# A four-layer graph network on one core: several joined edits, and an order planned with shorter delays

## The chip, the core and the metric

One core of a Trainium2 chip runs the whole program: TensorE (PE, with its weight loads PEld), VectorE (DVE), ScalarE (ACT), GpSimd (POOL) and SyncE (SP), which issues most DMAs. Each engine takes its instructions strictly in the order in which they stand in the program. The metric is the device time in microseconds of one execution; a median over several runs is given, and the profile shows one execution more.

## The reference, cut to what matters

The input x has 128 graphs of 64 nodes with 256 features, all with the same 64 x 64 adjacency adj. Four layers, each closed by a residual and a plain layer norm, all in f32:

```
x = LN(x + L0(x)); x = LN(x + L1(x)); x = LN(x + L2(x)); x = LN(x + L3(x))
L0: A_hat = D^-1/2 (adj + I) D^-1/2;  h = relu(BN((A_hat x) W1' + b1));  out = BN(h W2' + b2)
L1: Chebyshev-like: L_norm = 2 adj / (lam_max + 1e-8) - I, lam_max the largest eigenvalue of adj
    x1 = relu(LN((L_norm x) Wc + bc)) + x;  4-head attention masked by adj > 0;  LN;  GELU MLP;  LN
L2: two graph convolutions with relu, then for p = 1..4 an LSTM over windows of p nodes;
    the last state of each window replaces the node p-1 of the window
L3: Wh = h W;  e = leaky_relu(s1_i + s2_j), s1 = Wh a1, s2 = Wh a2, masked where adj == 0;
    softmax over j;  out = attention Wh
```

BN means over all 8192 rows, so layer 0 has two points at which every block must be done before any goes on.

## The kernel before, in words

The rows are cut into 16 blocks of 512 (eight graphs, as four tiles of 128 rows: `NT = 4`), and the blocks into four groups of four (`NG = 4`). A block is a [128, 1024] slab in SBUF, either row-major (`tm`) or feature-major (`fm`); TensorE transposes change one into the other (`to_fm`, `to_tm`). PSUM holds four slabs (`PS`), and eight spare slabs (`mem`), joined later by slabs that are no longer needed, carry what lives between two steps.

The program is not written in the order in which it runs. Each piece of work is a generator (`first_block`, `eig`, `second_block`, `end_block`, `block`, `gcn_block`, `unit`, which calls `lstm`, and `last_block`), and before each group of instructions it yields a `step`: the engine (T, V, S, G, or Q for SP's DMA queue), the planned duration, the PSUM slabs and the spare slabs that it takes, and, with `at`, the time at which its inputs are planned to be there. `flow` (lines 127-200) keeps a clock per engine, and picks again and again the step that can begin earliest, where MARGIN is added to the ready time of a step on T, V or S, and ties go to the stream with the lower priority number. A task's next step is planned 0.2 us after the end of the one before (`best[3] = end + 0.2`); where `at` is used, the body adds 0.2 by hand. What comes out is the order of instructions on each engine. Streams have a width: how many of their tasks may be open at once.

What the steps below touch:

- Start (lines 238-427): the four quadrants of `bdA` and `bdAT` (adj and its transpose twice on a diagonal) are loaded on SP in turn, `adj2` twice on ACT's queue, then x's first block and W1T on ACT's queue, W2T and six small columns on SP. VectorE makes the masks `cap1` and `cap3` and the degree `dinv`, and TensorE the matrix `AhT`, which the first aggregation (`aggregate`) waits for.
- `eig` (lines 432-487): 26 squarings of a 128 x 128 matrix for lam_max, spread between the matmuls of layer 0; `LnT` comes of it.
- Layer norms: `stats` (four times bn_stats and bn_aggr, then + EPS, lines 269-278), the power -1/2 on POOL, and then in `ln_steps` four VectorE operations (line 288), in `ln_steps_act` one small VectorE operation and four ScalarE ones (line 316), in `ln_affine_steps` eight VectorE ones.
- `end_block` ends layer 0, `block` is layer 1; both end with `ln_steps`. `gcn_block` is the convolutions of layer 2 with p = 1.
- `unit` runs p = 2, 3, 4 on a group, or part of it. Its first window step is plain. In the further steps the products of [x, h] with the weights use a seven-product form with sums of blocks (`product` at line 1000, stages 1 to 4): fewer columns on TensorE, and more copies and sums on ScalarE, VectorE and POOL. p = 4 of the last group is done as two units of 16 windows by 16 graphs (256 columns); all other units of p = 4 have 512.
- `last_block` (layer 3, lines 1269-1376) is done per block: add, norm, transpose, Wh (line 1308), e as 16 matmuls on quadrants of the array (1327, 1330), ScalarE 0.2 e (1337), VectorE max, mask, row maximum, subtraction (1340-1344), exp (1346), row sums and reciprocal, POOL's scaling (1352), transpose (1358), the product with Wh (1366), add (1370), norm, store.

In the second plan the streams are, from the most urgent: lending of slabs, small loads, weights, `last_block` of the last group (width 4), gcn (2), layers 0 end and 1 (6), units (2), `last_block` of the other groups (2).

Of the kernel before, what the change touches and what calls it, by code (L numbers as in the profile page):

```python
# [15 lines left out]
P = 128  # L16
# [3 lines left out]
NT = 4  # L20
# [7 lines left out]
EPS = 1e-5  # L28
MARGIN = {"T": 2.0, "V": 0.5, "S": 0.5}
# [3 lines left out]
def kernel(ctx: ExitStack, tc: tile.TileContext, a: dict, out: bass.AP):  # L33
# [93 lines left out]
    def flow(streams, margin):  # L127
# [8 lines left out]
        while True:  # L136
# [55 lines left out]
            best[5] += sl  # L192
            if waits:
                best[3] = end + 0.2
            try:
                best[2] = best[1].send(end)
# [43 lines left out]
    for s in range(2):  # L240
        h = halves[s]
        nc.sync.dma_start(bdA[h, h], a["adj"])
        nc.sync.dma_start(bdAT[h, h], a["adjT"])
        nc.scalar.dma_start(adj2[h, :], a["adj"])
        for m in (bdA, bdAT):
            G.memset(m[h, halves[1 - s]], 0.0)
# [9 lines left out]

    cap1 = ctile([P, N], "cap1")
    V.tensor_scalar(cap1, adj2, 0.0, BIG, ALU.is_gt, ALU.mult)
    V.tensor_scalar(cap1, cap1, -1.0e9, None, ALU.add)

    cap3 = ctile([P, N], "cap3")
    V.tensor_scalar(cap3, adj2, 0.0, 2.0, ALU.not_equal, ALU.mult)
    V.tensor_scalar(cap3, cap3, -1.0, BIG, ALU.add, ALU.mult)

# [4 lines left out]
    def stats(y, n=NT):  # L269

        st = sm.tile([P, n, 6], F32, tag="ln_st", name="ln_st")
# [8 lines left out]
    def ln_steps(y):  # L280

        yield step("V", 2.7)
# [9 lines left out]
    def ln_affine_steps(y, g, b):  # L292

        yield step("V", 2.7)
# [10 lines left out]
    def ln_steps_act(y):  # L305

        yield step("V", 2.7)
        mv, rs = stats(y)
        yield step("G", 1.0)
        G.tensor_tensor(rs, rs, neghalf[:, :NT], ALU.pow)  # L310
        yield step("V", 0.2)
        nm = sm.tile([P, NT], F32, tag="ln_nm", name="ln_nm")
        V.scalar_tensor_tensor(nm, mv[:, :, 0], -1.0, rs, ALU.mult, ALU.mult)  # L313
        yield step("S", 2.4)
        for t in range(NT):
            S.activation(  # L316
                y[:, t, :], y[:, t, :], AF.Identity, scale=rs[:, t : t + 1], bias=nm[:, t : t + 1]
            )
# [13 lines left out]
    def to_fm(ps, y):  # L332

        for c in range(2):
            for t in range(NT):
                T.transpose(ps[:, c, t * P : (t + 1) * P], y[:, t, c * P : (c + 1) * P], ident)

    def to_tm(ps, yT):

        for t in range(NT):  # L340
# [48 lines left out]
    with c0:  # L389
        ep = c0.enter_context(tc.tile_pool(name="eig", bufs=2))  # L390

        first = mem.take()
        nc.scalar.dma_start(tm(mem[first]), x_blk[0])
        W1T = load_w(wp, "W1T", a["L0_gnn_W1"], queue=nc.scalar)
        W2T = load_w(wp, "W2T", a["L0_gnn_W2"])
        cols = {k: load_col(wp, f"l0{k}", a[f"L0_gnn_{k}"]) for k in ("b1", "g1", "be1", "b2", "g2", "be2")}
# [11 lines left out]

        An = ctile([P, P], "An", wp)
        V.tensor_tensor(An, bdA, ident, ALU.add)  # L410
        tmp = etile("etmp")
        V.tensor_tensor(tmp, bdAT, ident, ALU.add)
        d3 = etile("d3", 3, 1)
        V.reduce_sum(d3[:, 0:1], An, axis=AX.X)
        V.reduce_sum(d3[:, 1:2], tmp, axis=AX.X)
        tmp = etile("etmp")
        V.tensor_tensor(tmp, An, ident, ALU.mult)
        V.reduce_sum(d3[:, 2:3], tmp, axis=AX.X)
        dinv = etile("dinv", 1, 1)
        V.tensor_tensor(dinv, d3[:, 0:1], d3[:, 1:2], ALU.add)  # L420
        V.tensor_tensor(dinv, dinv, d3[:, 2:3], ALU.subtract)
# [10 lines left out]
        def eig():  # L432
            Sy = etile("Sy", bufs=1)
            yield step("V", 1.2)
            V.tensor_tensor(Sy, bdA, bdAT, ALU.add)
# [75 lines left out]
        def first_block(i):  # L511
            if i:
# [3 lines left out]
            else:  # L516
                xs = first
            yield step("T", 1.9, ps=1, sl=1)
# [4 lines left out]
            yield step("V", 1.3, ps=-1)  # L523
# [3 lines left out]
            for hf in range(2):  # L527
                dst = fm(Xs[i]) if hf == 0 else H[i]
                yield step("T", 3.5, ps=1)
# [9 lines left out]
                yield step("V", 1.3, waits=hf == 1)  # L539
# [4 lines left out]
        def second_block(i):  # L544
# [5 lines left out]
            yield step("T", 7.0, ps=1)  # L550
# [14 lines left out]
            yield step("V", 1.3)  # L565
# [5 lines left out]
        tasks = [(None, lambda: first_block(0), 1), (None, eig, 0)]  # L571
        tasks += [(None, lambda i=i: first_block(i), 2) for i in blocks if i]
# [45 lines left out]
    def end_block(i):  # L618
# [9 lines left out]
        yield step("T", 1.0, ps=1)  # L628
# [3 lines left out]
        yield step("V", 1.3, ps=-1)  # L632
# [3 lines left out]
        yield from ln_steps(x)  # L636
        mark("end", i)

    def block(i):
        x = X[i]  # L640
        mark("begun", i)
        yield step("T", 1.9, ps=1, sl=1)
# [3 lines left out]
        yield step("S", 1.1, ps=-1)  # L646
        S.copy(mem[s_xp], PS[ps])
        PS.give(ps)
        yield step("T", 3.5, ps=1, sl=1)
# [4 lines left out]
        yield step("V", 1.3, ps=-1)  # L654
# [4 lines left out]
        yield step("V", 1.3)  # L659
        V.scalar_tensor_tensor(y, y, 0.0, x, ALU.max, ALU.add)  # L660

        yield step("T", 1.0, ps=1, sl=1)
# [3 lines left out]
        yield step("S", 1.1, ps=-1)  # L666
# [4 lines left out]
        for w in (Wq, Wk):  # L671
            yield step("T", 3.5, ps=1, sl=1)
# [3 lines left out]
            yield step("S", 1.1, ps=-1, waits=False)  # L676
# [23 lines left out]
        yield step("S", 1.1, ps=-1, waits=False)  # L700
# [8 lines left out]
        yield step("T", 1.9, ps=1, sl=1)  # L709
# [26 lines left out]
        yield step("S", 1.1, tbl="exp")  # L736
# [9 lines left out]
        yield step("T", 1.0, ps=1, sl=1)  # L746
# [6 lines left out]
        yield step("S", 1.1, ps=-1)  # L753
# [20 lines left out]
        yield step("S", 1.1, ps=-1)  # L774
        S.copy(mem[s_o], PS[ps])
        PS.give(ps)
        yield step("T", 3.5, ps=1)
# [3 lines left out]
        yield step("V", 1.3, ps=-1)  # L781
# [5 lines left out]
        yield step("T", 1.0, ps=1, sl=1)  # L787
# [14 lines left out]
        for hf in range(2):  # L802
            yield step("T", 3.5, ps=1, sl=1)
# [14 lines left out]
        yield step("T", 7.0, ps=1)  # L818
# [12 lines left out]
        yield step("V", 1.3, ps=-1)  # L831
# [4 lines left out]
        yield from ln_steps(x)  # L836
# [13 lines left out]
    av = load_w(gw, "av", a["L3_gnn_a"])  # L850
    bl = load_col(gw, "bih", a["L2_gnn_bih"])
# [3 lines left out]
    def gcn_rows():  # L855
# [5 lines left out]
        yield step("T", 1.0, ps=1)  # L861
# [40 lines left out]
    def lstm(p, n, parts, x_of, out_of):  # L902
# [38 lines left out]
        def gates(pair, t, ps, sl):  # L941
            t = yield step("S", 0.1 + n * 2.5e-3, ps=-1, at=t + 0.2, waits=False, tbl="sigmoid")
# [15 lines left out]
        for c in range(2):  # L958
# [3 lines left out]
            t = yield step("G", g_us, at=t + 0.2, waits=False)  # L962
# [567 lines left out]
```

## Time and profile before

| | us |
|---|---|
| runs shown: median (lowest to highest) | 2455.06 (2454.82 to 2457.53) |
| profiled execution: its own time | 2454.4 |
| profiled execution: span on the core | 2452.6 |
| TensorE busy | 2353.9 |
| VectorE busy | 1274.4 |
| ScalarE busy | 1095.9 |
| GpSimd busy | 572.8 |
| mean granted TensorE clock | 0.982 of full speed |

In the profile L12 is line 12 of the kernel; lines of helpers (L324 aggregate, L342 and L336 transposes, L348 and L360 weight products) stand for all their callers. In a table by stage each row has the stretch, its length, then busy us and number of instructions of PE, PEld, DVE, ACT and POOL, the granted clock, the DMA share and GB/s. In the list of waits a row reads "engine, what it was to compute and its line <- what it waited for: us in total, times, longest". In a timeline a row has the start, the time taken, the engine, the line, the operation, and the idle time before it in brackets. Ends of matmuls are modelled; their starts are what to count with.

### The profile page before, as it was taken

What the parts mean: (1) busy time and instruction counts of PE and PEld (TensorE: products, weight loads), DVE (VectorE), ACT (ScalarE), POOL (GpSimd) and SP (SyncE); (2) the same over time, 40 slices, a digit from 0 to 9 for tenths busy, and PEclk for the clock granted to TensorE, in tenths of its full rate; (3) what the DMA queues carried; (4) which work ended last, traced back from release to release, by engine and by line L of the source; (5) the groups of instructions that cost most, each with busy time, mean ns of one, the idle gap of its engine ahead of it and who ended that gap; (6) DMA issues with size and microseconds to landing.
All of it is one profiled execution on the core that took longest, in us unless ns stands there. A gap on an engine that the chain in (4) does not pass through costs nothing. (4 is left out here: it accounts for less than half of the span.)

```text
span 2452.6 us, 35349 instructions
## 1 busy us (share of the span) xinstructions
PE 2353.9 (96%) x14468; PEld 1818.8 (74%) x14468; DVE 1274.4 (52%) x2965; ACT 1095.9 (45%) x1916; POOL 572.8 (23%) x416
## 2 busy tenths in 40 slices
PE   8999888999999999999999999999999999999986
PEld 5544466767667767675766888899999889888874
DVE  4542387657455645484552433345344455455664
ACT  2256332333444343434434444445435465556774
POOL 0000034233323222343132222222222221222211
PEclk9999899999999999999999999999999999999997
DMA  5110110100000000000100000000000010000111
GB/s 171 43 52 0 40 36 27 44 3 15 1 9 10 18 9 10 1 9 35 44 26 11 16 1 1 1 18 1 1 1 18 1 35 10 26 18 18 61 53 44
DMA packets 40499, 57.60 MB, mean 23 GB/s; under 512 B 4624, under 2 KB 33936, under 8 KB 40336
## 3 DMA queue, kind: packets, MB, share of 16 engines
q1 hardware_dynamic: 39376, 54.25, 6.8%
q8 instruction: 113, 1.85, 0.3%
q10 hardware_dynamic: 960, 1.08, 0.1%
q14 instruction: 50, 0.41, 0.1%
HBM read 38.55 MB, written 16.78 MB: 23 GB/s over the span
## 5 line engine op out<-in xcount | busy, mean ns | idle before, releaser
L1000 PE MATMUL ps<-x,x 128*128 128x256 f32 (+1 forms) x1024 | 228.4, 360 | 0.0
L1000 PEld LDWEIGHTS ps<-x,x 128*128 128x128 f32 x1024 | 179.8, 190 | 19.5 <-DVE t L1046 0.4
L1000 PE MATMUL ps<-t,x 128*128 128x256 f32 (+1 forms) x800 | 178.5, 359 | 1.4 <-ACT x L1040 1.4
L1000 PEld LDWEIGHTS ps<-t,x 128*128 128x128 f32 x800 | 140.5, 190 | 18.9 <-ACT x L1040 2.0
L932 PE MATMUL ps<-h,wL 128*128 128x144 f32 (+2 forms) x552 | 131.8, 393 | 0.0
L348 PE MATMUL ps<-t,W1T 128*128 128x512 f32 x256 | 116.0, 597 | 0.0
L932 PEld LDWEIGHTS ps<-h,wL 128*128 128x128 f32 x552 | 87.9, 190 | 37.7 <-issue 36.8
L285 POOL TENSOR_TENSOR ln_rs<-ln_rs,neghalf 128x4 f32<-128x4 f32 x48 | 49.6, 1033 | 202.1 <-DVE ln_rs L277 202.0
L944 ACT ACTIVATE t<-ps,bih 128x512 f32<-128x512 f32 (+3 forms) x116 | 68.5, 642 | 57.7 <-PE ps L932 57.6
L275 DVE BATCH_NORM_STATS2 ln_st<-x 128x6 f32<-128x256 f32 x240 | 92.0, 403 | 0.7
L1059 DVE COPY x<-ps 128x256 f32<-128x256 f32 (+3 forms) x84 | 30.7, 366 | 118.6 <-PE ps L1000 118.5
L297 POOL TENSOR_TENSOR ln_rs<-ln_rs,neghalf 128x4 f32<-128x4 f32 x32 | 36.6, 1145 | 230.9 <-DVE ln_rs L277 230.8
L1076 ACT ACTIVATE x<-x,bih 128x512 f32<-128x512 f32 (+3 forms) x84 | 53.1, 632 | 77.9 <-DVE x L1066 77.7
L932 PE MATMUL ps<-h,x 128*128 128x256 f32 x384 | 87.1, 379 | 0.8 <-ACT t L1152 0.8
L1000 PE MATMUL ps<-h,x 128*128 128x256 f32 (+1 forms) x416 | 84.4, 333 | 1.1 <-DVE x L1059 0.6
L932 PEld LDWEIGHTS ps<-h,x 128*128 128x128 f32 x384 | 72.7, 190 | 10.9 <-ACT t L1152 1.2
L348 PEld LDWEIGHTS ps<-t,W1T 128*128 128x128 f32 x256 | 46.2, 191 | 45.9 <-issue 45.9
L288 DVE TENSOR_SCALAR x<-x,ln_mv,ln_rs 128x256 f32<-128x256 f32 x144 | 63.3, 495 | 31.5 <-POOL ln_rs L285 31.5
L1066 DVE TENSOR_TENSOR x<-ps,x 128x512 f32<-128x512 f32 (+3 forms) x84 | 48.5, 579 | 57.4 <-PE ps L1000 46.1
L1076 ACT ACTIVATE t<-t,bih 128x512 f32<-128x512 f32 (+3 forms) x59 | 36.9, 629 | 86.1 <-DVE t L1066 85.9
L944 ACT ACTIVATE x<-ps,bih 128x512 f32<-128x512 f32 (+3 forms) x88 | 51.6, 639 | 50.2 <-PE ps L932 50.1
L276 DVE BATCH_NORM_AGGREGATE ln_mv<-ln_st 128x2 f32<-128x6 f32 x448 | 71.5, 166 | 0.0
(663 smaller groups left out, 5691.6 us busy)
## 6 DMA issues: line engine op xcount, KB each, us to landing
t<-in_x_dram SPq DMA_DIRECT2D x25, 512.0 KB, 4.0
xd<-x SPq DMA_DIRECT2D x16, 512.0 KB, 2.6
x<-xd SPq DMA_DIRECT2D x8, 512.0 KB, 3.3
out_dram<-x SPq DMA_DIRECT2D x8, 512.0 KB, 2.9
h<-in_x_dram SPq DMA_DIRECT2D x6, 512.0 KB, 4.1
t<-xd SPq DMA_DIRECT2D x6, 512.0 KB, 3.3
out_dram<-t SPq DMA_DIRECT2D x6, 512.0 KB, 2.9
wL<-in_L_gnn_Wih_dram SPq DMA_DIRECT2D x2, 1024.0 KB, 5.0
```

The lines of the kernel that those rows point to most:

```text
L275: V.bn_stats(st[:, t, :], y[:, t, :])
L276: V.bn_aggr(mv[:, t, :], st[:, t, :])
L285: G.tensor_tensor(rs, rs, neghalf[:, :NT], ALU.pow)
L288: V.tensor_scalar(y[:, t, :], y[:, t, :], mv[:, t, 0:1], rs[:, t : t + 1], ALU.subtract, ALU.mult)
L297: G.tensor_tensor(rs, rs, neghalf[:, :NT], ALU.pow)
L348: T.matmul(ps[:, c, :], w[:, k, (off + c) * P : (off + c + 1) * P], yT[:, k, :], start=(k == 0), stop=(k == nk - 1),)
L932: T.matmul(spread(fm(PS[ps])[:, j, :n], q), WL[p][0][:, k, m], x_of(0, q)[:, k], start=(k == 0), stop=(k == 1),)
L944: S.activation(of(sl)[:, j], fm(PS[ps])[:, j, :n], AF.Tanh if g == 2 else AF.Sigmoid, bias=bias(g, c))
L1000: T.matmul(dst, WS[p][name](k, g), y[:, k], start=first and k == 0, stop=k == 1, skip_group_check=not first)
L1059: V.tensor_copy(y[:, 1, :], v[:, 0, :])
L1066: V.tensor_tensor(y[:, 0:2, :], v[:, 2:4, :], y[:, 0:2, :], ALU.add)
L1076: S.activation(of(act[g])[:, 0], of(act[g])[:, 0], f, bias=bias(g, 0))
```

## The change

1. Planner: `end + 0.2` becomes `end + lag`, 0.2 after a step on T and 0.06 after any other; the 0.2 that the bodies added by hand are gone, since `send` now gives `end + lag`. Many planned durations are a little shorter.
2. Start: bdAT is loaded on ACT's queue; adj2 is summed from the halves of bdA instead of loaded; three blocks of x are loaded ahead (SP, ACT, SP); all columns but b1, and W2T, are loaded by a task of their own (`later_loads`), which also makes the masks; the degree comes of two operations with an accumulated row sum.
3. `end_block` and the last norm of `block` use `ln_steps_act`.
4. Units of 16 graphs (the last two) run `plain_steps` instead of the seven-product form.
5. `last_block` can do part of a block; the last group is done in halves of two tiles. e comes of two matmuls over the whole array: block-diagonal ones times a diagonal made by POOL, and the identity times a broadcast column. leaky_relu is one VectorE operation after the mask, the subtraction of the maximum is the bias of exp, the row sums are accumulated by exp, and the division comes with the last add.
6. Streams: the last two units have a stream of their own, and `last_block` of the first three groups has width 4.

```diff
+LAG, LAG_T = 0.06, 0.2
...
+            lag = LAG_T if e == "T" else LAG
             if waits:
-                best[3] = end + 0.2
+                best[3] = end + lag
             try:
-                best[2] = best[1].send(end)
+                best[2] = best[1].send(end + lag)
...
-        nc.sync.dma_start(bdAT[h, h], a["adjT"])
-        nc.scalar.dma_start(adj2[h, :], a["adj"])
+        nc.scalar.dma_start(bdAT[h, h], a["adjT"])
...
-        yield from ln_steps(x)
+        yield from ln_steps_act(x)
         mark("end", i)
...
+        early = [mem.take() for _ in range(3)]
+        for i, q in enumerate((nc.sync, nc.scalar, nc.sync)):
+            q.dma_start(tm(mem[early[i]]), x_blk[i])
+            if i == 1:
+                W1T = load_w(wp, "W1T", a["L0_gnn_W1"], queue=nc.scalar)
...
+        V.scalar_tensor_tensor(Sy, bdA, 1.0, bdAT, ALU.mult, ALU.add, accum_out=d3[:, 0:1])
+        V.scalar_tensor_tensor(tmp, bdA, 1.0, ident, ALU.mult, ALU.mult, accum_out=d3[:, 1:2])
+        V.scalar_tensor_tensor(dinv, d3[:, 0:1], 1.0, d3[:, 1:2], ALU.add, ALU.subtract)
...
+        if len(parts) == 1 and p > 1:
+            yield from plain_steps(p, n, us, of, bias, x_of, lambda ap: spread(ap, 0), last_h, s_cell, s_h, h_at)
+            return
...
+            def products(pair):
+                t = yield step("T", 8 * us, ps=1, sl=1, at=h_at - 2 * us, waits=False)
+                ps, sl = PS.take(), mem.take()
+                for j, (g, c) in enumerate(pair):
+                    m = slice(g * D + c * P, g * D + (c + 1) * P)
+                    dst = fm(PS[ps])[:, j, :n]
+                    for k in range(2):
+                        T.matmul(shaped(dst), WL[p][0][:, k, m], x[:, k], start=(k == 0), stop=False)
+                    for k in range(2):
+                        T.matmul(dst, WL[p][1][:, k, m], of(s_h)[:, k], start=False, stop=(k == 1))
...
+        G.tensor_tensor(d, bc_mid(unit2, nt), bc_last(s12[:, :nt, 1], N), ALU.mult)
+        T.matmul(pe, bdones, d, start=True, stop=False)
+        T.matmul(pe, ident, bc_last(s12[:, :nt, 0], N), start=False, stop=True)
+        V.tensor_tensor(e, pe, bc_mid(cap3, nt), ALU.min)
+        V.scalar_tensor_tensor(e, e, 0.2, e, ALU.mult, ALU.max)
+        V.reduce_max(mx[:, :nt], e, axis=AX.X)
+        V.tensor_scalar(mx[:, :nt], mx[:, :nt], -1.0, None, ALU.mult)
+        for t in range(nt):
+            S.activation(e[:, t, :], e[:, t, :], AF.Exp, bias=mx[:, t : t + 1], accum_out=sums[:, t : t + 1])
...
+        for t in range(nt):
+            V.scalar_tensor_tensor(
+                x[:, t, :], tm(PS[ps])[:, t, :], sums[:, t : t + 1], x[:, t, :], ALU.mult, ALU.add
+            )
...
+    last = [last_of(i) for i in range(early)]
+    end = [last_of(i, t, 2) for i in range(early, NBLK) for t in range(0, NT, 2)]
...
-            Stream(4, 2, last[early:]),
+            Stream(4, 2, end),
...
-            Stream(2, 5, units),
-            Stream(2, 6, last[:early]),
+            Stream(2, 5, units[:-2]),
+            Stream(2, 5, units[-2:]),
+            Stream(4, 6, last),
```

## The prediction

> **What bounds the kernel now.** I read the busy time by stage first, because the shares over the whole span (TensorE 96%) hide where the loss is.
>
> ```profile
> core 0: us, PE busy (x) PEld busy (x) DVE busy (x) ACT busy (x) POOL busy (x), PEclk, DMA share, GB/s
> 0.00:281.00 281.00, 266.39 (x882) 142.21 (x882) 112.99 (x245) 106.02 (x161) 3.54 (x16) 0.99 0.20 58
> 281.00:540.00 259.00, 226.18 (x1623) 166.35 (x1622) 182.52 (x478) 96.06 (x117) 83.06 (x54) 0.92 0.11 35
> 540.00:2280.00 1740.00, 1724.75 (x10756) 1398.71 (x10755) 880.32 (x1911) 786.58 (x1426) 454.94 (x313) 1.00 0.04 14
> 2280.00:2377.00 97.00, 86.97 (x805) 75.86 (x804) 62.05 (x204) 67.29 (x145) 20.19 (x21) 1.00 0.17 55
> 2377.00:2453.00 76.00, 49.65 (x408) 35.62 (x408) 36.50 (x129) 39.95 (x71) 11.11 (x13) 0.77 0.11 36
> ```
>
> From 540 to 2280 TensorE is busy 99% of the time at full clock: there only TensorE work counts. The losses are 33 us idle and some 20 us of lowered clock (259 x 0.08) in 281-540, where VectorE has 182 us to do and ScalarE 96, and 26 us idle plus 17 us of clock (76 x 0.23) after 2377, where the last recurrence matmul (L1000) has gone by. The head loses 10 us. The waits of TensorE name who is late:
>
> ```profile
> PE ps L426 <- DVE etmp L424: 10.2, 1, 10.2
> PE ps L1358 <- POOL wL L1352: 7.6, 1, 7.6
> PE ps L348 <- DVE t L782: 6.3, 1, 6.3
> PE ps L324 <- DVE t L832: 5.2, 1, 5.2
> ...
> PE ps L336 <- DVE x L633: 4.1, 1, 4.1
> ```
>
> Lines 782, 832 and 633 lie in 281-540: VectorE is the late one. The 7.6 us of L1358 lie in the last 20 us, where the chain is one block's own latency.
>
> **Rates.** The timeline of TensorE gives the step from one matmul record to the next (each f32 matmul leaves two):
>
> ```profile
> 2182.16 1.03 PE L1000 MATMUL ps<-t,x 128*128 128x256 f32 x4
> 2183.02 0.61 PE L1000 MATMUL ps<-h,wB 128*128 128x128 f32 x4
> 2183.47 0.83 PE L1000 MATMUL ps<-x,x 128*128 128x128 f32 x5
> ```
>
> Four records of 256 columns take 0.86 us (0.216 each), four of 128 take 0.45 (0.112 each).
>
> **1. TensorE work.** In the last two units (p=4, group 3, 256 columns) the seven-product form gives way to the plain one. Per unit and step it was 4 gates x 7 products x 2 = 56 matmuls of 128 columns, 112 records x 0.112 = 12.5 us; it is 8 chunks x 4 = 32 matmuls of 256, 64 x 0.216 = 13.8. Two units of three steps: +7.8 us. Their first step has the same columns: 0. The score matrix e was 16 quadrant matmuls per block (L1327, L1330), from 2345.12 to 2346.25 in the timeline, 1.13 us x 16 = 18.1; now two matmuls over all rows, 4 x 0.216 = 0.86 for each of 12 full blocks and 4 x 0.112 = 0.45 for each of 8 half blocks, 13.9: -4.2. Sum +3.6 us, on the bound. ScalarE and VectorE do less per plain step (no copies and differences, L1038-1068), which hides nothing and costs nothing here.
>
> **2. Head.** VectorE waits for the second bdAT until 7.07 (issued fourth on SP, at 2.62); TensorE starts at 10.15. Now bdAT goes out on ACT's queue where the dropped adj loads stood; those had landed at 3.85. In the built order ten VectorE operations lie before the dinv power as before, four of them the cheap cap ones that are moved in behind Sy: 2.05 us then, about 1.8 now. Start 4.2 + 1.8 + 1.0 = 7.0: -3. Moved loads: x0, x1 and x2 now go ahead of W1T, 2 MB in all, at the 236 GB/s of the first 20 us landed by 11; W1T is wanted after three aggregations, some 7 us after 8.3, at 15. The column loads and W2T stand behind on SP, W2T wanted at 160. So hidden; were W1T late by its 5.0 us of landing, the gain would be gone. Bounds -3.5 to +2; I take -3.
>
> **3. Normalisation moved from VectorE to ScalarE** (end_block and the second norm of block). VectorE's four operations of L288 take 1.38 us, ScalarE's four of L316 2.08 plus 0.17 for ln_nm on VectorE:
>
> ```profile
> 301.25 1.01 POOL L285 TENSOR_TENSOR ln_rs<-ln_rs,neghalf 128x4 f32<-128x4 f32 x1 [6.09 <-DVE ln_rs L277]
> 302.29 1.38 DVE L288 TENSOR_SCALAR x<-x,ln_mv,ln_rs 128x256 f32<-128x256 f32 x4 [1.12 <-POOL ln_rs L285]
> ...
> 2423.51 2.08 ACT x L316 x4
> ```
>
> Here a rule speaks against the change. The Trainium skill, "ScalarE: Activation LUTs", Rules for kernel authors, gives adds and multiplies to VectorE, not ScalarE; by the rule each of 32 norms gets 0.9 us slower, +28 us were all on the path. The stage row decides otherwise: VectorE drops 64 operations of x in 281-540, 29.0 us of records, for 16 x 0.17, so 182 becomes about 156 of 259; ScalarE goes from 96 to 129. Only the first block, alone in the pipe, pays its 0.9. VectorE is busy 29.6 of 30 us in 310-340 and 8.8 of 10 in 380-390, where the gaps lie. I give back the first gap of 4.1, 2.5 each of the 6.3 and 5.2 (two norms of 1.2 lie before each), 1.5 of the rest: 10.6. The clock: TensorE runs at 0.50 in 320-325 and 0.62 in 325-330 behind the 4.1 us gap, 4.4 us lost. "TensorE: Matmul & The Clock Gate", Part 1, has the clock halved after some 3.4 us of idling until as long a busy window has passed, which would make 1.7 us of it; the row shows 4.4, and I take the row. 10.6 + 4.4 - 0.9 = -14. Bounds: 0 (ScalarE's queue is in order, and a norm behind an eviction holds the next aggregation) and -35 (all 23 us of gaps from 303 to 540 and 12 of clock).
>
> **4. Order and end.** LAG, the step durations and the streams issue nothing; what they cost is the order that comes out, read from the built program. There, the last recurrence matmul is followed on TensorE by 62 us of work: 56 L1308-type (24.2), 64 L1366-type (0.117 a record, 15), 96 transposes (10.7), 64 of L1358 (5.2), 20 for e (6.9). Before it is 37. So 25 us leave the time before that point: it comes at 2377 - 3 - 14 + 3.6 - 25 = 2339. What is late next is ScalarE: after the last tanh its queue holds about 64 us: 56 norms x 0.53 back to back (29.7), 14 copies of 0.58 (8.1), eight of L1278's kind (6.5), eight xT copies (6.3), ten aT copies (3.3), 32 exps of 64 columns, one table load (1.3). Those exps have no row; the nearest, 128 columns with a bias, take 0.37-0.40 (L1080, L1078), and the formula of "ScalarE: Activation LUTs", What ACT_TABLE_LOAD costs, makes 0.24 back to back: 8 to 12 us, 8.6 taken, since queued they overlap. At what share can it work? Before, with about three blocks in flight, 40 of 76 us, 0.53; VectorE with several tasks in 310-340, 0.99. With up to eight tasks I take 0.78: 82 us, plus 4 from the last matmul to the last h and 4 from ScalarE's last operation to the end (2448.7 to 2452.6): 90. On POOL the diagonal product (L1417) has the size of the e product dropped (L1352, 0.61): 0; it stands behind the norms' power of 1.03, and what waits for it is that block's e. SP issues four more loads and four more stores of half size, 0.5 each; a store waiting for its norm holds the load behind it, which here is two full blocks of group 2 near the end; that is part of the 0.78. Fewer table loads (65 to 61) are free, ScalarE not being the bound before.
>
> Sum, on the profiled span: 2339 + 90 = 2429. The median of the runs (2455.06) lies 2.5 above the span (2452.6), so **2431**.
>
> **Rivals.**
> The fill gains nothing: the waits on VectorE turn into waits on ScalarE at the same place. For it: lines 625 and 316 share one queue. Against: ScalarE is idle 63% there. 2431 + 14 = 2445.
> The end is bound tighter and the fill empties: share 0.9 (79 us for the end, -11) and -25 in the fill: 2409.
> A slower kernel, one mechanism: work is put behind the recurrence and ScalarE doesn't keep up. Six blocks' worth starts when the last h is there, group 2's full blocks last, in in-order queues on all engines. At the old share of 0.53 the end takes 64/0.53 + 8 = 129 us, 39 more than taken: 2470. It decides where the share falls below 0.59: 64/0.59 + 8 = 116, 2431 + 26 = 2457.
> Nothing comes of it: shorter planned delays only permute what is bound by TensorE, and the 3.6 us of added work eats the head: 2453-2457.
>
> **Chances.** Main case 0.46, fill gains nothing 0.20, tight end 0.12, nothing 0.08, slower 0.14. A repeat of this kernel can't tell less than 0.2% (5 us) from no change: faster is 0.46 + 0.20 + 0.12 = 0.78 of it, same 0.08, slower 0.14. The main case alone spans 2418-2444. Range for 8 in 10: 2410 (the tight end) to 2457 (where the slower case begins).
>
> **What would show it.** Right: first matmul near 7; in 281-540 VectorE below 160 us of work and TensorE idle near 22; TensorE's clock 0.95 there; last recurrence matmul near 2339; ScalarE about 0.78 busy from then on. Wrong: waits of TensorE on L316's kind as long as those on L633 and L782; the 540-2280 stretch no longer at 99%; after the last recurrence matmul more than 112 us, or ScalarE near half busy there.

## The result, and the profile after

The changed kernel takes 2448.08 us (median, 2446.94 to 2449.05), the kernel before, beside it, 2455.23: a ratio of 0.9969, 95% interval 0.9957 to 0.998. It is faster, by 7 us where 24 were forecast. The profiled execution has a span of 2447.3 us.

The table by stage of the changed kernel, with the columns explained above (length, busy us of PE, PEld, DVE, ACT, POOL, granted clock, DMA share, GB/s):

```profile
0.00:281.00 281.00, 267.69 (x882) 142.99 (x882) 114.22 (x247) 106.88 (x161) 3.56 (x17) 0.99 0.20 60
281.00:540.00 259.00, 234.96 (x1698) 174.35 (x1698) 175.35 (x466) 133.76 (x191) 87.18 (x61) 0.95 0.11 35
540.00:2280.00 1740.00, 1721.05 (x10294) 1386.87 (x10295) 827.50 (x1800) 808.21 (x1485) 442.34 (x307) 1.00 0.04 13
2280.00:2377.00 97.00, 88.44 (x503) 70.24 (x502) 55.58 (x207) 65.59 (x146) 20.61 (x28) 0.95 0.15 50
2377.00:2448.00 71.00, 50.41 (x328) 33.37 (x326) 36.17 (x151) 37.70 (x105) 11.97 (x16) 0.84 0.16 52
```

In 281-540 TensorE's idle time fell from 32.8 to 24.0 us and its clock rose from 0.92 to 0.95 (259 x 0.03 = 7.8 us): 16.6 us, forecast 14. TensorE's waits and its timeline show the rest of the way, and where the last recurrence matmul (L1161 now) stands:

```profile
PE ps L438 <- DVE etmp L436: 6.7, 1, 6.7
PE ps L344 <- ACT h L823: 5.8, 1, 5.8
PE ps L332 <- DVE t L671: 4.3, 1, 4.3
PE ps L488 <- DVE ed L485: 3.8, 1, 3.8
```

```profile
2334.55 1.03 PE L1022 MATMUL ps<-t,x 128*128 128x256 f32 x4
...
2338.00 1.03 PE L1161 MATMUL ps<-x,x 128*128 128x256 f32 x4
2338.86 0.59 PE L1421 MATMUL ps<-wA,bdones 128*128 128x256 f32 x2
```

The first wait ends where TensorE starts: 6.7 us instead of 10.2. The second is new, in 540-600: ScalarE is the late one there now. The fourth stands at the end of layer 0, where TensorE waits for the last sums of the eigenvalue (before, 0.6 us at the same place). After 2338.9 no recurrence is left: the forecast for this point was 2339. Before, the same point was at 2376.7 (the last four records began at 2376.21 and take 0.45), so 37.8 us were gained up to it:

```profile
2376.21 0.71 PE L1000 MATMUL ps<-h,x 128*128 128x128 f32 x4 [0.48 <-DVE x L1068]
```

What is behind it takes 2447.3 - 2338.9 = **108.4 us, 75.9 before**: 32.5 us of the 37.8 are given back. The row of that stretch, from 2340.1 on, has ScalarE at 66.3 of 107.2 us, a share of 0.62:

```profile
2340.10:2447.30 107.20, 78.98 (x500) 54.19 (x498) 61.28 (x255) 66.33 (x169) 20.17 (x27) 0.85 0.14 45
```

L1022 in the timeline above belongs to the third group's last unit. It ends 3.5 us before the last group's units do, and so layer 3 of the third group begins as late as that of the last.

### The profile page after: what moved, and what is told of

Same layout as the page of the kernel before. It is cut to its first block, busy times and chain, and to the rows that moved or that the text cites. A ratio compares the mean times of both kernels' runs of the same rounds, so it can differ in the third digit from the quotient of the medians.

```text
span 2447.3 us, 33911 instructions
## 1 busy us (share of the span) xinstructions
PE 2362.6 (97%) x13700; PEld 1807.8 (74%) x13700; DVE 1208.8 (49%) x2868; ACT 1152.1 (47%) x2086; POOL 565.7 (23%) x426
## 4 chain that ended last, share of the span: by engine, by line
PE 73%; DVE 6%; ACT 4%; POOL 2%; issue 1%; POOLq 0%; ACTq 0%; DVEq 0%
PE ps L1022 24%; PE ps L950 13%; PE ps L344 10%; PE ps L356 5%; PE ps L833 4%; PE ps L320 3%; PE ps L703 2%; PE ps L1397 2%; PE ps L1159 2%; PE ps L1161 2%; DVE ln_st L270 1%; PE ps L332 1%; PE ps L776 1%; PE ps L1450 1%; ACT x L312 1%
## 5 line engine op out<-in xcount | busy, mean ns | idle before, releaser
L1022 PE MATMUL ps<-x,x 128*128 128x256 f32 x832 | 203.2, 379 | 0.7 <-DVE x L1090 0.7
L1022 PEld LDWEIGHTS ps<-x,x 128*128 128x128 f32 x832 | 155.0, 190 | 19.9 <-issue 1.1
L312 ACT ACTIVATE x<-x,ln_nm,ln_rs 128x256 f32<-128x256 f32 x176 | 92.9, 592 | 112.8 <-DVE ln_nm L309 112.8
L1022 PE MATMUL ps<-t,x 128*128 128x256 f32 x576 | 137.7, 380 | 0.0
L1022 PEld LDWEIGHTS ps<-t,x 128*128 128x128 f32 x576 | 108.4, 190 | 14.5 <-issue 0.4
L306 POOL TENSOR_TENSOR ln_rs<-ln_rs,neghalf 128x4 f32<-128x4 f32 (+1 forms) x72 | 69.4, 964 | 189.7 <-DVE ln_rs L272 167.9
L950 PE MATMUL ps<-t,wL 128*128 128x512 f32 x216 | 94.5, 594 | 1.8 <-ACT t L1248 1.8
L292 POOL TENSOR_TENSOR ln_rs<-ln_rs,neghalf 128x4 f32<-128x4 f32 x32 | 35.9, 1122 | 239.5 <-DVE ln_rs L272 239.0
L950 PE MATMUL ps<-h,x 128*128 128x256 f32 x384 | 86.8, 379 | 0.0
L344 PE MATMUL ps<-t,wA 128*128 128x512 f32 x176 | 81.5, 608 | 2.6 <-ACT t L679 2.6
L1022 PE MATMUL ps<-h,x 128*128 128x256 f32 x320 | 82.5, 380 | 0.0
L950 PEld LDWEIGHTS ps<-h,x 128*128 128x128 f32 x384 | 72.8, 190 | 10.2 <-issue 0.5
L950 PE MATMUL ps<-h,wL 128*128 128x192 f32 (+2 forms) x432 | 79.8, 338 | 0.0
L1098 ACT ACTIVATE x<-x,bih 128x512 f32<-128x512 f32 (+2 forms) x65 | 42.2, 650 | 76.2 <-DVE x L1088 73.9
```

The lines of the kernel that those rows point to most:

```text
L306: G.tensor_tensor(rs, rs, neghalf[:, :n], ALU.pow)
L312: S.activation(y[:, t, :], y[:, t, :], AF.Identity, scale=rs[:, t : t + 1], bias=nm[:, t : t + 1])
L344: T.matmul(ps[:, c, :], w[:, k, (off + c) * P : (off + c + 1) * P], yT[:, k, :], start=(k == 0), stop=(k == nk - 1),)
L950: T.matmul(spread(fm(PS[ps])[:, j, :n], q), WL[p][0][:, k, m], x_of(0, q)[:, k], start=(k == 0), stop=(k == 1),)
L1022: T.matmul(dst, WS[p][name](k, g), y[:, k], start=first and k == 0, stop=k == 1, skip_group_check=not first)
```

## The experiments

Below, "the point" is the end of the last recurrence matmul in the profiled execution, "behind" the time from there to the end of the span, and "work behind" the TensorE work that follows the point in the built order, at the rates of the trace before (0.216 us a record of 256 columns, 0.112 of 128).

| run | median us | ratio to before (95%) | work behind | point | behind |
|---|---|---|---|---|---|
| before | 2455 to 2456 | 1 | 36.8 | 2376.7 | 75.9 |
| the changed kernel | 2448.08 | 0.9969 (0.9957-0.998) | 61.0 | 2338.9 | 108.4 |
| e1 one stream | 2425.66 | 0.9878 (0.9864-0.9891) | 26.9 | 2379.2 | 45.8 |
| e2 pair last | 2462.64 | 1.0027 (1.0016-1.0039) | 17.0 | 2418.6 | 42.2 |
| e3 seven-product | 2433.14 | 0.9908 (0.9895-0.9922) | 30.4 | 2380.6 | 50.1 |
| e4 norms on VectorE | 2472.89 | 1.007 (1.0057-1.0082) | 61.0 | 2363.9 | 108.4 |
| e5 before, two streams | 2495.16 | 1.016 (1.0146-1.0174) | 60.1 | 2359.1 | 135.9 |
| e6 e1, width 2 | 2459.56 | 1.0015 (1.0008-1.0022) | 52.5 | 2351.8 | 106.6 |
| e7 e1, seven-product | 2451.62 | 0.9985 (0.9978-0.9991) | 19.4 | 2401.0 | 48.8 |
| e8 before, norms on ScalarE | 2479.42 | 1.0102 (1.0086-1.0117) | 36.8 | 2397.3 | 75.7 |
| e9 delay 0.07 | 2450.55 | 0.9979 (0.9972-0.9987) | 60.1 | 2344.0 | 104.8 |
| e10 e1, delay 0.07 | 2438.76 | 0.9932 (0.992-0.9945) | 34.5 | 2378.6 | 58.4 |
| e11 e1, delay 0.2 | 2455.73 | 1.0001 (0.9993-1.0009) | 22.6 | 2404.3 | 48.4 |
| e12 e1, whole blocks | 2432.89 | 0.9909 (0.9895-0.9922) | 32.8 | 2370.7 | 60.5 |
| e16 delay 0.2 | 2463.22 | 1.0034 (1.002-1.0049) | 53.6 | 2366.7 | 94.6 |

### Where the gain went: e1, e2, e5, e6

**e1** puts the last two units back into the common stream.

```diff
-            Stream(2, 5, units[:-2]),
-            Stream(2, 5, units[-2:]),
+            Stream(2, 5, units),
```

> The changed kernel with one edit: all units in one stream of width 2 again, as before the change. In its built order about 27 us of TensorE work follow the last recurrence matmul, instead of 61 in the changed kernel and 37 in the kernel before. Theory (the gain up to that point was real and was given back because layer-3 work was put behind the recurrence, where ScalarE reaches only a share of 0.62 to 0.65): the point comes about 34 us later, near 2373, and the time behind it falls faster than that. Before, 37 us of work took 75.6 us; after, 61 took 108; by that line 27 take about 62. Span 2435, median 2436, 12 us below the changed kernel. Rival (the share is low because four tasks of the new last_block interleave in in-order queues, whatever stands behind the recurrence): the time behind it stays near 100 us, 2470. Rival (work is only shifted, what leaves the end is added before it and nothing else): 2448, as the changed kernel.

Measured: 2425.66 us, 22 below the changed kernel and 30 below the kernel before; the fastest of all. TensorE's timeline and the stretch row of e1:

```profile
2302.56 1.13 PE L1022 MATMUL ps<-t,x 128*128 128x256 f32 x4
```

```profile
2378.34 1.03 PE L1161 MATMUL ps<-wA,x 128*128 128x256 f32 x4
2379.20 1.91 PE L1397 MATMUL ps<-Wx,wA 128*128 128x258 f32 x8
```

```profile
2380.44:2425.00 44.56, 32.72 (x228) 23.08 (x226) 29.41 (x127) 32.04 (x86) 10.71 (x17) 0.87 0.18 59
```

The third group's unit (L1022) now ends at 2303, 76 us before the point, so its layer 3 runs between the recurrence's steps. The point is 40 us later (34 expected) and what is behind is 62.6 us shorter: 1.8 us for each of the 34.1 us of TensorE work no longer there. Ahead of the point a moved us costs about 1.2 us (40.3 for 34.1); behind it 1.8. ScalarE's share is 32.0 of 44.6 us, 0.72: not a constant of the code, as the rival with the interleaving had it.

**e2** makes the last two units less urgent than the other groups' layer 3.

```diff
-            Stream(2, 5, units[-2:]),
             Stream(4, 6, last),
+            Stream(2, 7, units[-2:]),
```

> The changed kernel with one edit: the stream of the last two units comes behind the stream of the other groups' last_block, so that the latter is more urgent. About 17 us of TensorE work follow the last recurrence matmul (61 in the changed kernel). Theory (work put behind the recurrence is the cost): by the line through 37 us of work in 75.6 us and 61 in 108, 17 take about 49 us; the last recurrence matmul comes 44 us later, near 2383; span 2432, median 2433. Rival (work behind the recurrence is the cheap place for it, because without it the last two units' steps run with nothing beside them): TensorE idles between the steps from 2280 on, the last recurrence matmul comes near 2400, and the time is 2450 or more.

Measured: 2462.64 us; the rival has the number right. Behind the point 42.2 us remain (49 expected), but the point is at 2418.6. The row of e2 from 2200 to there, and TensorE's longest waits in it:

```profile
2200.00:2419.83 219.83, 198.02 (x1042) 159.75 (x1041) 93.18 (x313) 121.94 (x268) 35.12 (x41) 0.94 0.12 39
```

```profile
PE ps L332 <- ACT t L312: 4.1, 1, 4.1
PE ps L1450 <- ACT wA L1444: 3.7, 1, 3.7
PE ps L1442 <- ACT wA L1434: 2.7, 1, 2.7
PE ps L1442 <- ACT t L1434: 2.5, 1, 2.5
```

TensorE idles 21.8 us there and loses 13 more of clock (220 x 0.06). But some 20 of the 21.8 us are waits of layer-3 instructions for their own norms, exps and copies, and little over 1 us is a wait of the recurrence. The more urgent layer 3 stands ahead of the recurrence in the queues: in one step ScalarE's tanh (L1181) starts at 2401.17, though VectorE began the sum that it takes at 2393.99 and needed 0.42 us; norms and exps of layer 3 stand between. So the reason of the rival, steps with nothing beside them, is not what the trace shows.

**e5** is the kernel before with the separate stream alone (`Stream(2, 5, units)` split as in the change).

> The kernel before with one edit alone: its last two units get a stream of their own, as in the change. In the built order 60 us of TensorE work then follow the last recurrence matmul, instead of 37. Theory (work put behind the recurrence costs more there than it frees before it; the changed kernel against e1 gives 108.4 - 46.6 = 61.8 us more behind the point for 34 us of TensorE work moved, 1.8 us for each): the last recurrence matmul comes near 2376 - 23 = 2353, the time behind it grows from 75.6 to about 117, span 2470, some 17 us slower than before. Rival (the cost belongs to the changed last_block with its halves and width 4): the time behind grows by about 23, within 4 us of before.

Measured: 2495.16 us, 40 slower than before. The point is 17.6 us earlier (23 expected), and the time behind grows by 60 us for 23.3 us of work, 2.6 for each. So the edit costs by itself, without the new layer 3. That it costs more with the old one may come of the more steps that one's blocks take; this wasn't tried. Its row behind the point:

```profile
2360.78:2495.00 134.22, 80.04 (x660) 58.51 (x656) 64.46 (x223) 60.57 (x109) 19.39 (x22) 0.76 0.12 42
```

ScalarE is busy 0.45 of that stretch and TensorE 0.60.

**e6** is e1 with width 2 for layer 3 of the first groups (`Stream(4, 6, last)` to `Stream(2, 6, last)`).

> e1 (all units in one stream) with one more edit: last_block of the first three groups has width 2 again. 52.5 us of TensorE work follow the last recurrence matmul, 27 in e1. Theory (only the amount of work behind it counts, 0.8 us net for each us moved): the point comes near 2353 and the time behind is about 93, median 2446. Rival (width 4 interleaves tasks and makes each late, width 2 works better for the same amount): median 2430 or less.

Measured: 2459.56 us, 34 above e1, where 20 were expected; behind the point 106.6 us for 52.5 of work, about as much as the changed kernel takes for 61 with width 4. The rival falls: width 4 is worth having, in the stretch and for what it brings ahead of it.

### How much one order says: e9, e10, e12

**e9** and **e10** change the planned delay of the changed kernel and of e1 by 0.01 us (`LAG` 0.06 to 0.07).

> A control: the changed kernel with the planned delay 0.07 instead of 0.06 us. Nothing else changes, but a plan reacts to the least shift, so a different order comes out, with 60 us of TensorE work behind the last recurrence matmul (61 in the changed kernel). Theory (the end's cost goes by the amount of work behind the last recurrence matmul): 2448 within 5 us. Rival (the order of the plan as such moves the time by more than the changes tested, so that the single comparisons so far mean little): anything further than 10 us from 2448.

> The same control on e1: one stream for all units, planned delay 0.07. 34.5 us of TensorE work follow the last recurrence matmul (27 in e1). Theory (0.8 us net for each us behind it): 2426 + 6 = 2432, within 5 us. Rival (e1's gain was luck of one order): 2440 or more.

Measured: 2450.55, 2.5 above the changed kernel, as expected; and 2438.76, 13.1 above e1, between the two expectations. In e10 the work behind rose by 7.6 us and the time behind by 12.6; the point came no earlier, as TensorE's busy time in 1000-1400 fell from 395.2 to 388.0 us. So one plan's luck is at least 13 us here, by two trials, and no single comparison of two kernels below that says anything of the edit between them. e1 beats e10 by its order alone; both beat the changed kernel. The separate stream can be judged by four pairs that differ in it alone: with it the time is longer by 22 us (changed kernel and e1), 12 (e9 and e10), 7 (e16 and e11, below) and 40 (e5 and before), and each us of work that it puts behind the point adds 1.5 to 2.6 us there.

**e12** is e1 with the last group in whole blocks.

```diff
-    end = [last_of(i, t, 2) for i in range(early, NBLK) for t in range(0, NT, 2)]
+    end = [last_of(i) for i in range(early, NBLK)]
```

> e1 with the last group's last_block in whole blocks again. 32.8 us of TensorE work follow the last recurrence matmul. Theory (halves shorten the last chain, and the amount behind the point is larger): by 0.8 us for each of 6 us and some 10 us more of latency for the last whole block, 2440. Rival (halves are worth nothing: twice as many small steps queue on VectorE and ScalarE): 2428 or less.

Measured: 2432.89 us, 7 above e1: between the expectations, and less than the control moved. What the halves are worth stays open.

### The plain steps: e3, e7

Both take back the plain steps of the last two units, e3 in the changed kernel and e7 in e1: without these lines the unit has two parts again, and goes by the seven-product code.

```diff
-        if nb < BG:
-            parts = [(slice(0, 2 * hn), nw)]
```

> The changed kernel with one edit: the last two units run the seven-product form again, as before the change. TensorE has about 8 to 10 us less to do, and in the built order only about 30 us of work follow the last recurrence matmul. Theory (displaced work): that point comes near 2339 + 31 - 9 = 2361, the time behind it falls to about 67, median 2429. Rival (the plain steps shorten the last units' chain: fewer stages on ScalarE and VectorE between two steps, which matters once TensorE has little else to fill with): TensorE idles before the last recurrence matmul, it comes at 2375 or later, median 2445 to 2455.

> e1 with one more edit: the last two units run the seven-product form again. TensorE has 10.4 us less to do and 19 us of work follow the last recurrence matmul, 27 in e1. Theory (TensorE's work is the bound up to that point): it comes near 2378 + 8 - 10 = 2376, the time behind is about 43 (as with 17 us of work in e2): median 2419. Rival (with the others' work used up, the units' own chain sets the point, and the seven-product form has the longer chain, as e3 hints, whose point came with e1's although it had about 14 us less to do before it): TensorE idles more from 2280 on, the point comes near 2390, median 2432 or more.

Measured: e3 2433.14, 15 below the changed kernel; e7 2451.62, 26 above e1. e3 comes near the time of its theory (2429), but not by its parts: the new order leaves 30 us of work behind the point and not 61, and 50.1 us pass there (67 expected), while the point is at 2380.6 and not at 2361. In e7 it is at 2401.0, 22 later than in e1, with 3 us less TensorE work ahead of it. The row of e7 from 2200 to its point:

```profile
2200.00:2402.61 202.61, 186.18 (x1315) 161.02 (x1314) 108.34 (x355) 131.35 (x327) 42.86 (x45) 0.97 0.11 37
```

TensorE idles 16 us there at a clock of 0.97; in e1 5.6 us (174.8 busy of 180.4) at 1.00. Of e7's waits there, 7.1 us are products (L1022) waiting for the copies and gates that the seven-product form has on ScalarE (L1062, L1102). The seven-product form has less TensorE work and the longer chain per step, and at the end the chain is what counts; e7's 26 us are above the control, e3's 15 hardly.

### The norms: e4, e8

**e4** puts the norms of `end_block` and the last ones of `block` back to VectorE in the changed kernel, **e8** moves only them to ScalarE in the kernel before.

```diff
-        yield from ln_steps_act(x)
+        yield from ln_steps(x)
```

> The changed kernel with one edit: the norms of end_block and the last ones of block go back to four VectorE operations each. Theory (the gain of about 16 us between 281 and 540 came from VectorE's relief): VectorE has about 182 us to do there again, TensorE idles above 30 us at a clock near 0.92, and the time is about 2448 + 16 = 2464. Rival (the gain there came from the new order with its shorter delays): idle stays near 24 us, the time within 4 us of 2448.

> The kernel before with one part of the change alone: the norms of end_block and the last ones of block by ScalarE. Theory (this part gives the whole gain between 281 and 540): VectorE about 155 us there, TensorE idle about 22, clock 0.95, and the whole about 14 us faster than before, 2441. Rival (it takes the new order as well, as e4 lost 25 us and not 16 by undoing it): less than 5 us faster, 2450 or more.

Measured: e4 2472.89, 25 above the changed kernel; e8 2479.42, **24 above the kernel before**. The rival's "2450 or more" covers e8's number, but neither expectation had a loss. The stage rows of e8, and of the kernel before for the same stretches:

```profile
281.00:540.00 259.00, 235.81 (x1681) 169.34 (x1681) 174.95 (x467) 134.19 (x193) 89.57 (x58) 0.94 0.12 35
...
700.00:1000.00 300.00, 292.77 (x1977) 199.81 (x1978) 166.07 (x338) 130.01 (x165) 95.36 (x54) 0.99 0.03 10
1000.00:2200.00 1200.00, 1174.94 (x6917) 998.10 (x6915) 553.93 (x1158) 556.08 (x1094) 287.90 (x206) 0.99 0.04 14
```

```profile
700.00:1000.00 300.00, 300.00 (x1986) 207.68 (x1985) 159.74 (x361) 126.06 (x148) 87.14 (x53) 1.00 0.03 10
1000.00:2200.00 1200.00, 1186.42 (x7004) 1006.68 (x7004) 570.98 (x1195) 548.09 (x1088) 293.20 (x210) 1.00 0.04 14
```

In 281-540 e8 gains what the prediction put there: 9.6 us of idle time and 259 x 0.02 = 5.2 of clock, 14.8. But the point comes 20.6 us later than before, so some 35 are lost behind that stage. Up to 2200 TensorE idles some 22 us more, and the clock is 0.99 where it was 1.00. The timelines of TensorE, ScalarE and VectorE in e8 at one of those gaps:

```profile
1137.82 2.50 PE L324 MATMUL ps<-bdAT,x 128*128 128x128 f32 x10 [5.78 <-ACT x L1145]
```

```profile
1136.71 1.06 ACT L1145 ACTIVATE x<-x 128x1024 f32<-128x1024 f32 x1 [11.54 <-DVE x L1142]
```

```profile
1135.40 0.17 DVE L276 BATCH_NORM_AGGREGATE ln_mv<-ln_st 128x2 f32<-128x6 f32 x1
1135.48 1.19 DVE L1142 TENSOR_TENSOR x<-ps,rb 128x1024 f32<-128x1024 f32 x1
```

TensorE waited 5.8 us for a relu on ScalarE, which had itself stood idle 11.5 us for an eviction on VectorE (L1142), whose turn came behind the statistics and norms of two other blocks (L275 to L303). The work is the same as before; the plan, with other durations, put it in another order. In e4 the loss lies behind 540 too, as its rows show:

```profile
281.00:540.00 259.00, 235.85 (x1675) 170.78 (x1677) 189.45 (x502) 99.94 (x121) 87.24 (x60) 0.93 0.11 34
540.00:1000.00 460.00, 444.78 (x3040) 310.91 (x3035) 278.62 (x622) 169.68 (x198) 143.88 (x86) 0.98 0.03 10
```

In 281-540 VectorE has its work back (189 us), but TensorE idles 23.2 us, as in the changed kernel (24.0), and not above 30 as the theory had it; only the clock falls, from 0.95 to 0.93. In that stage the rival is nearly right. In 540-1000 TensorE is busy 444.8 of 460 us (455.9 in the changed kernel), at a clock of 0.98 instead of 0.99.

### The shorter delays: e11, e16

e11 sets `LAG` back to 0.2 in e1, e16 in the changed kernel (a step on T has 0.2 in all).

> e1 with the planned delay after steps of VectorE, ScalarE, GpSimd and the DMA queue at 0.2 us again. 22.6 us of TensorE work follow the last recurrence matmul. Theory (the delay only permutes the order, and the amount behind the point decides): 2425 within 5 us. Rival (the shorter delays are what fills TensorE before 2280, as real delays are shorter than 0.2): TensorE idles some 10 us more between 281 and 2280, 2435 or more.

> The changed kernel with the planned delay at 0.2 us for all engines again. 53.6 us of TensorE work follow the last recurrence matmul (61 in the changed kernel). Theory (shorter delays fill TensorE, 27 us in e11): the point comes some 7 + 27 us later, near 2373, the time behind it falls to about 95: 2468. Rival (e11 was one unlucky order): within 10 us of 2448.

Measured: e11 2455.73, 30 above e1, the point 25 us later; e16 2463.22, 15 above the changed kernel, the point 27.8 later and 13.8 less behind it. The row of e11:

```profile
540.00:1000.00 460.00, 442.45 (x2948) 305.21 (x2947) 238.44 (x525) 192.62 (x239) 138.62 (x82) 0.99 0.02 9
```

TensorE is busy 12.4 us less in 540-1000 than in e1 (454.8). A likely reason is that a task's next step comes too far down the queues when its delay is planned too long; no run shows it. The point moves by 25 to 28 us in both kernels, but these are hardly two trials: in 540-1000 both are busy 442.5 us, with much the same order. What speaks against the rival (one unlucky order) is that the control moved the point by 5.1 us at most; the 15 us of e16's time alone would be too near the control's 13.

### What limits the stretch behind the point: e13, e14, e15

Each takes part of one engine's work out of `last_block`, at planned durations left as they are: e13 and e14 norm, or take statistics of, every fourth column only, e15 leaves out the second product of each pair of Wh. The diff is shortened: the value 4 stands where the kernels have a parameter.

```diff
-                y[:, t, :], y[:, t, :], AF.Identity, ...      # e13
+                y[:, t, ::4], y[:, t, ::4], AF.Identity, ...
-            V.bn_stats(st[:, t, :], y[:, t, :])               # e14
+            V.bn_stats(st[:, t, :], y[:, t, ::4])
-                for k in range(2):                            # e15
+                for k in range(1):
```

> The changed kernel, in which last_block's norms write every fourth column only (the rest of each row is left as it was, so that part of the computation is left out). ScalarE has 52 such operations behind the last recurrence matmul, 0.594 us each; with 64 columns about 0.34 (as the exps of 64 columns there): some 13 us less. Theory of the prediction (ScalarE's queue bounds that stretch): it falls from 108 by about 13/0.62 = 20 us, to 88. Rival (a chain through all engines, on which these operations have 9.3 us): by about 4 us. Rival (TensorE bounds it): 0 to 2.

> The changed kernel, in which last_block's norms take their statistics from every fourth column (three quarters are left out of mean and variance). VectorE has 52 bn_stats behind the last recurrence matmul, 0.403 us each; with 64 columns an estimated 0.15 to 0.2: some 11 us less. Theory of the prediction (ScalarE): 0. Rival (a chain through all engines, on which bn_stats has 8.7 us): about 5 us less than 108. Rival (VectorE bounds the stretch, being full in 2360-2370): 10 or more.

> The changed kernel, in which Wh takes only the first 128 of the 256 features (the second product of each pair is left out). TensorE has 12 us less behind the last recurrence matmul and 16 us less before it. Theory of the prediction (ScalarE): the stretch stays at 108. Rival (a chain through all engines, on which these products have 16.4 us): about 8 us less. Rival (TensorE bounds it, 79 of 107 us busy at a clock of 0.85): 12/0.85 = 14 us less, or more.

The stretch rows of e13, e14 and e15, in this order, each from 2.1 us behind the start of its last recurrence matmul:

```profile
2338.69:2440.20 101.51, 75.40 (x500) 52.09 (x498) 61.05 (x255) 60.86 (x169) 20.17 (x27) 0.88 0.14 47
```

```profile
2340.17:2438.70 98.53, 73.59 (x500) 50.97 (x498) 53.83 (x255) 66.82 (x169) 20.20 (x27) 0.91 0.15 49
```

```profile
2327.02:2429.10 102.08, 65.32 (x444) 42.85 (x442) 60.62 (x255) 66.83 (x170) 20.16 (x27) 0.86 0.14 47
```

Against the 107.2 us of the changed kernel: e13 takes 5.5 us from ScalarE (13 were meant) and the stretch is 5.7 shorter; e14 takes 7.5 from VectorE, 8.7 shorter; e15 takes 13.7 from TensorE, 5.1 shorter. The whole times are 2442.08, 2439.81 and 2429.65 us; of e15's, 13 us were gained ahead of the point. One us taken from ScalarE gives 1.0, from VectorE 1.2, from TensorE 0.4. If ScalarE's queue alone were the bound, e14 and e15 would have given nothing; the theory of the prediction falls. So does TensorE as the only bound, for e13 and e14 gain with its work as it was. Of e14's rivals VectorE as the bound (10 us or more) and the chain (5) lie on both sides of its 8.7, but e13 and e15 gain with VectorE's work as it was. What fits all three is a chain through the engines, whose records stand in this trace in the order of the program. The chain of waits of the changed kernel has them in turn (the x4 of L1434 are two exps, each with the read of its sum):

```profile
2372.51 0.31 DVE ln_st L270
2372.82 0.07 DVE ln_mv L271
...
2374.04 1.02 POOL ln_rs L306
2375.06 0.02 issue
2375.08 0.16 DVE ln_nm L309
2375.25 0.09 DVE mx L1430
2375.36 0.77 ACT x L1434 x4
2376.13 1.97 ACT h L312 x4
```

Statistics of several blocks queue on VectorE, then come POOL's power, a small VectorE operation, exps and norms on ScalarE, then TensorE. Of the 103 us listed from 2340 on, TensorE has 42, VectorE 29, ScalarE 22, POOL with its queue 6.

## Why the prediction was right or wrong

- **Head (-3).** The first matmul starts 3.5 us earlier, and layer 0's last product ends at 277.5 instead of 280.0. Then the new wait of 3.8 us (L488) takes most of it back: 882 matmul records begin before 281 in both kernels, and of the idle time up to there only 1.3 us are saved. What may last of the head is part of the next stage's number.
- **TensorE work (+3.6).** That the plain steps cost only their 7.8 us of TensorE work was right for the kernel as it is; that ScalarE and VectorE doing less there "hides nothing" was not: e7 without them has its point 22 us later.
- **Norms (-14).** The stage gave 16.6, near the forecast (VectorE 175 us in the row and not below 160, as more work was drawn into it: TensorE has 1698 records there, 1623 before). That the norms gave it isn't shown. They suffice in the kernel before (e8, 14.8), but in the changed kernel the stage keeps some 12 of the 16.6 without them (e4: 9.6 us of idle time and 259 x 0.01 of clock against before). Nor does the stage's gain last to the end by itself: e8 loses more behind it. What the norms do for the changed kernel shows in 540-1000. TensorE idles 4.1 us there; with the norms back on VectorE 15.2 (e4), with delays of 0.2 17.5 (e16), with the norms on ScalarE alone 11.5 (e8), and 1.4 in the kernel before, which has neither. In these orders the two edits belong together; each is one order, so how far this is luck stays open. The rival "the fill gains nothing" was wrong in its stage.
- **The point (2339).** It came at 2338.9, but that close by luck. By the rows, 0-281 gave -1.3, 281-540 -16.6, and the work +3.6 and -24.2 (moved behind). Two terms stand in the prediction at nothing, and nearly cancel. In 540-2280 idle time rose by 3.7 us (19.0 instead of 15.3), and some 6 us of clock were lost, of which the first two rows below show 3.4 and 3.0. From 2280 to the point idle time fell from 10.0 us to 0.2 (third row). In sum -38.2 of rounded terms, measured -37.8.

```profile
540.00:560.00 20.00, 15.85 (x40) 8.35 (x41) 9.42 (x20) 11.51 (x15) 6.54 (x4) 0.83 0.00 1
1200.00:1220.00 20.00, 17.07 (x126) 13.59 (x125) 17.14 (x53) 5.43 (x8) 8.84 (x6) 0.85 0.07 27
2280.00:2338.90 58.90, 58.67 (x326) 48.35 (x325) 30.47 (x102) 35.76 (x81) 12.41 (x17) 1.00 0.20 63
```

- **The end (90 us): the step that failed.** It took ScalarE's 64 us of work at a share of 0.78. The work was sized right in sum (66.3 in the row from 2340.1, though in it the exps, with the reads of their sums, take 11.6 us and not 8.6), the share is 0.62, and the stretch took 108.4, which is 18.4 more: 2429 + 18 = 2447, the measured span. What was wrong is the model and not only its number. I divided one queue's work by a share chosen between those of two other stretches; the stretch is bound by a chain through several in-order queues, in which ScalarE, VectorE and TensorE each have a part (e13 to e15). TensorE's own 62 us also came out as 79 us of records, at a clock of 0.85.
- **The slower rival.** Its mechanism, work put behind the recurrence, is what happened, short of its break-even (116 us at a share of 0.59). e5 shows it in full in the kernel before: +40 us.
- **"Nothing comes of it: shorter delays only permute".** Wrong as far as e11 and e16 go: with delays of 0.2 the point comes 25 to 28 us later.

Up to the point the change is worth 38 us, or 14 if the 24 that only moved are left out; the separate stream for the last two units then costs it 22 of what one line less would keep (e1).

## What to carry to other kernels

Where a long recurrence holds the bounding engine full, the end is to be read as two numbers: when the last recurrent step ends, and how much other work stands behind it. Here 17 to 30 us of work behind took 42 to 50 us (e1, e2, e3, e7, e11), which hardly falls with the work and so may be mostly one block's own latency, and each us that the separate stream added cost 1.5 to 2.6. Work taken from behind the point must not be put ahead of the recurrence in the queues (e2). An edit that helps one stage of a planned program has to be judged on the whole order, since e8 won its stage and lost the run, and a control with a meaningless shift of the plan tells how large a difference must be to mean anything: more than 13 us here.

## What the hardware showed unexpectedly

A quarter of the columns is far from a quarter of the time: ScalarE's norm of 256 columns takes 594 ns in the records, of every fourth one (64) still about 500, while the exp of 64 columns side by side takes 337; VectorE's bn_stats goes from 403 to 255 ns. Here is the row of the norm from 2335 on, of e13:

```profile
L312 ACT ACTIVATE h<-h,ln_nm,ln_rs 128x64 f32<-128x64 f32 x28 | 12.5, 504 | 7.5 <-DVE ln_nm L309 7.5
```

Whether the stride or the function makes the difference between 504 and 337 wasn't tried. And the sum that exp accumulates has a price: each exp leaves a second record on ScalarE that reads it, as the timeline of the changed kernel shows:

```profile
2375.36 0.35 ACT L1434 ACTIVATE x<-x,mx 128x64 f32<-128x64 f32 x1 [0.62 <-DVE mx L1430]
2375.61 0.19 ACT L1434 ACTIVATION_READ_ACCUMULATOR x<-x,mx 128x1 f32 x1
2375.71 0.33 ACT L1434 ACTIVATE x<-x,mx 128x64 f32<-128x64 f32 x1
```

From one exp to the next it is 0.35 us, within the estimate of 0.24 to 0.40 that the prediction allowed for, and above the 0.27 that it took (8.6 us for 32). The formula's 0.24 fits the exp alone, whose read starts 0.25 us after it; the read adds 0.10.
